# Row sums of banded attention on 64-row tiles in two PSUM banks, with fixed banks in the band steps

## The chip, the cores and the metric

The kernel runs on one core of a Trainium2 chip. TensorE (PE) multiplies matrices and writes only to PSUM, an accumulator memory of eight banks of 512 fp32 columns per partition; VectorE (DVE) and ScalarE (ACT) read PSUM and work elementwise; GpSimd (POOL) works on SBUF; SyncE (SP) issues the transfers. The metric is the time of the whole program on the device in microseconds, a median of runs; lower is better.

## The reference

The input x has the shape (2, 256, 128, 128): batch B, time T, frequency FB, channels C. Three layers follow one another, each with a residual:

```python
xt = _ln(x, ln_t_w, ln_t_b).transpose(0, 2, 1, 3)
x = x + _mha(xt, t_wi, t_bi, t_wo, t_bo, 4, causal_mask(256)).transpose(0, 2, 1, 3)
xf = _ln(x, ln_f_w, ln_f_b)
x = x + _mha(xf, f_wi, f_bi, f_wo, f_bo, 4, band_mask(128, 16))   # |i - j| <= 16
xn = _ln(x, ln_n_w, ln_n_b)
x = x + gelu(xn @ w1.T + b1) @ w2.T + b2                          # 128 -> 512 -> 128
```

All values are fp32. Attention has four heads of 32 channels; a softmax weight is the exponential of a score divided by the sum of the exponentials over the keys. In the second layer a query sees only the keys within 16 places, so a query among the first 48 of 128 sees only the first 64 keys, a query among the last 48 only the last 64, and the 32 in the middle see keys of both halves.

## The kernel before

The work is cut into groups of four tiles of 128 tokens (512 columns). There are three kinds. `OverTime` (128 groups) computes attention over time and comes first. Then follow 16 runs; each has eight `OverBands` groups (attention over frequency, called B1 to B8 here) and then eight `FeedForward` groups (F1 to F8). `run` (line 1263) writes the order of the instructions out by hand: step n issues the first half of group n, the weighted sums (`weigh`) of group n-1, and the output product of group n-2, besides loads and normalisations of later groups and the queries, keys and values of group n+1. Each engine keeps exactly this order (`InOrder`, line 894), and waits on the others by semaphores.

In a band step PE does, in this order: the scores of the group (`OverBands.scores`, line 775: keys times queries, 32-row by 64-column tiles, 80 queries for each half of the keys); the row sums and the weighted values of the group before (`weigh`, line 814: `rp` and `op`); the output product of the one before that (`output`, line 630: `yp`); then the queries, keys and values of the next group (`queries_keys`, `values`). ACT makes the exponentials into the tile `pf`, then for the group before the logarithm of the sums (`ln`) and its exponential (`r`, a first estimate of the reciprocal), then copies queries, keys and values out of PSUM. POOL cuts the band of three heads of `pf` by two selects each; DVE adds the band mask of the fourth to its scores before the exponential ("bank<-bank,band" in the profile). DVE then, in its order: normalises a later group (four "xh"), transposes it ("z"), adds the output to the residual (`finish`, line 636, "x<-bank,x"), and in `divide` (line 615) refines the reciprocal ("bank<-bank,r", "u") and multiplies the weighted values by it ("oT"). In steps B4 to B6 the statistics of F1 to F3 follow, in B8 those of F4; their root (`rstd`) is computed by POOL.

At the turn, step F1, both halves of the hidden products are issued first, then the sums of B8, whose reciprocal is taken exactly (`invert_exactly`, line 610, one DVE RECIPROCAL), then the output of B7 and its `finish`, which stands behind the RECIPROCAL in DVE's order. Step F2 issues half of its hidden products ("xnT,w1f" in the profile), the second product of F1 ("w2T_sb,hT", into `zp`), the other half of the hidden products, and the output of B8.

In the steps of bands and feed-forward every PSUM tile takes the next of the eight banks in turn (`bank`, line 944, and `turn_of_bank`, line 940), with one or two banks set aside ahead for the output and the next queries (`held`, `follow`). A bank that is written again waits for those who still read it. The product that makes all 512 columns of a head's row sums is one matrix multiplication with a matrix of ones: 128 keys, 32 output rows, 512 queries.

Of the kernel before, what the change touches and what calls it, by code (L numbers as in the profile page):

```python
# [19 lines left out]
P = 128  # L20
H = 4
# [11 lines left out]
BANK = 512  # L33
HALF = P // 2
LARGE = 1e20
EXP_SET = "natural_log_exp_and_others"


# [520 lines left out]


class Attention(Group):
    which = None
    swapped = ()
    place = {}
# [6 lines left out]
    def queries_keys(self):  # L571
        path = self.path
        wf = path.k.wf[self.which]
        self.qp = path.bank([P, NT * P], "qp", self.place.get("qp", path.held.pop("qp", None)))
# [27 lines left out]
    def invert(self):  # L602

        path = self.path
        ln = path.work.tile([P, NT * P], F32, name="ln", bufs=2)
        path.scalar.activation(ln, self.rp, AF.Ln)
        self.r0 = path.work.tile([P, NT * P], F32, name="r0", bufs=2)
        path.scalar.activation(self.r0, ln, AF.Exp, scale=-1.0)

    def invert_exactly(self):  # L610
        self.r0 = None
        self.r = self.path.work.tile([P, NT * P], F32, name="ln", bufs=2)
        self.path.vector.reciprocal(self.r, self.rp)

    def divide(self):

        path, vector = self.path, self.path.vector
        if self.r0 is None:
            self.oT = path.work.tile([P, NT * P], F32, name="oT", bufs=2)
            u = path.work.tile([P, NT * P], F32, name="u", bufs=2)  # L620
            vector.tensor_tensor(by_rows(u), by_tile(self.op), by_tile(self.r), ALU.mult)
            vector.tensor_scalar(self.oT, u, -1.0, None, ALU.mult)
            return
        vector.tensor_tensor(self.rp, self.rp, self.r0, ALU.mult)
        u = path.work.tile([P, NT * P], F32, name="u", bufs=2)
        vector.scalar_tensor_tensor(u, self.rp, 2.0, self.r0, ALU.subtract, ALU.mult)
        self.oT = path.work.tile([P, NT * P], F32, name="oT", bufs=2)
        vector.tensor_tensor(by_rows(self.oT), by_tile(self.op), by_tile(u), ALU.mult)

    def output(self):  # L630
        path = self.path
        self.yp = path.bank([P, NT, P], "yp", self.place.get("yp", path.held.pop("yp", None)))
# [9 lines left out]
def rows_of(h):  # L642
    return slice(h * D, (h + 1) * D)
# [124 lines left out]
class OverBands(Attention):  # L768


    which = 1
    follow = ("yp",)
    by_vector = 1

    def scores(self, heads):
        path = self.path
        self.sp = {h: path.bank([P, NT * P], "sp") for h in heads}
        for i in range(NT):
            for e in range(2):
                keys = slice(e * HALF, (e + 1) * HALF)  # L780
                a = i * P + e * (HALF - BAND)
                q = slice(a, a + HALF + BAND)
                for h in heads:
                    r = rows_of(h)
                    path.tensor.matmul(
                        self.sp[h][keys, q], self.kT[r, i * P + e * HALF : i * P + (e + 1) * HALF], self.qT[r, q],
                        start=True, stop=True,
                    )
# [24 lines left out]

    def weigh(self):
        path = self.path

        path.held = {name: path.turn_of_bank() for name in self.follow}
        self.rp = path.bank([P, NT * P], "rp")
        for h in range(H):
            path.tensor.matmul(  # L820
                self.rp[rows_of(h), :], path.k.ones[:, 0:D], self.p[:, h].rearrange("p i q -> p (i q)"),
                start=True, stop=True,
            )
        self.op = path.bank([P, NT * P], "op")
        for i in range(NT):
            c = slice(i * P, (i + 1) * P)
            for h in range(H):
                r = rows_of(h)
                path.tensor.matmul(self.op[r, c], self.v[:, i, r], self.p[:, h, i, :], start=True, stop=True)


class FeedForward(Group):
# [36 lines left out]
    def weigh(self):  # L869
        path, NI = self.path, self.path.k.NI  # L870
        if self.last:
            zp = [path.bank([P, P], "zp") for i in range(NT)]
        else:
            self.zp = path.bank([P, NT, P], "zp")
            zp = [self.zp[:, i] for i in range(NT)]
        self.zps = zp
        for i in range(NT):
            for j in range(NI):
                product(
                    path, zp[i], self.hT[:, j, i * P : (i + 1) * P], path.k.w2T[:, j, :],  # L880
                    start=(j == 0), stop=(j == NI - 1),
                )
# [26 lines left out]
class BoundedPath:  # L909
    def __init__(self, ctx, tc, k):  # L910
        self.tc, self.nc, self.k = tc, tc.nc, k
        self.xpool = ctx.enter_context(tc.tile_pool(name="xpool", bufs=3))
        self.work = ctx.enter_context(tc.tile_pool(name="work", bufs=3))
        self.small = ctx.enter_context(tc.tile_pool(name="small", bufs=6))
        ps = ctx.enter_context(tc.tile_pool(name="ps", bufs=1, space=PSUM))
        self.ps = [ps.tile([P, BANK], F32, name=f"bank{i}", tag=f"bank{i}") for i in range(8)]
        self.next_bank = 0
        self.inputs = 0
        self.held = {}
# [12 lines left out]
        self.band = once.tile([P, P], F32, name="band")  # L932
        tc.nc.gpsimd.memset(self.band, 0.0)
        for s in (1, -1):
            tc.nc.gpsimd.affine_select(
                out=self.band, in_=self.band, compare_op=ALU.is_ge, fill=-1e30, base=BAND,
                pattern=[[-s, P]], channel_multiplier=s,
            )

    def turn_of_bank(self):  # L940
        i, self.next_bank = self.next_bank, (self.next_bank + 1) % 8
        return i

    def bank(self, shape, name, i=None):

# [317 lines left out]
    def run(self, x, out):  # L1263
# [7 lines left out]
        def at(n, kind):  # L1271
            return 0 <= n < len(groups) and isinstance(groups[n], kind)
# [3 lines left out]
                do(n, *names)  # L1276


        for i in range(len(groups) - 2):
            if at(i, OverBands) and at(i + 1, OverBands):  # L1280
                groups[i].follow = ("yp", "qp")
# [15 lines left out]

        ff = [i for i in range(len(groups)) if at(i, FeedForward)][2:]

        self.start(groups)  # L1300
        for n in range(len(groups) + 2):
            feeds = [at(n - 2 + i, FeedForward) for i in range(5)]
# [2 lines left out]
            old, new = (groups[i] if at(i, OverTime) else None for i in (n, n + 1))  # L1305
            if bands[2] and feeds[1]:
                self.scalar.preload_act_table_set(EXP_SET)
            if n + 4 in early:
                do(n + 4, "root")
            do(n, "first_half", "first_function", "first_mask")  # L1310
            if n == 0:
                do(3, "normalize_flat")
            if 2 < n < 6:
# [3 lines left out]
            if old is not None or new is not None:  # L1317
                time_scores(old, new)
                b = self.banks
                Attention.place = dict(yp=b["b0"], rp=b["b3"], op=b["a1"], qp=b["a2"], kp=b["b1"], vp0=b["b0"], vp1=b["b2"])  # L1320
            else:
                Attention.place = {}
            if old is not None:
                old.second_weights(old.late)
                if n + 2 < TURNED:
# [175 lines left out]
```

## Time and profile before

| what | us |
|---|---|
| median of 3 runs | 2636.74 (2636.16 to 2640.02) |
| the profiled execution, its own time | 2633.24 |
| its span, first to last instruction | 2631.4 |
| PE busy | 2618.3 (100%) |
| DVE busy | 2140.6 (81%) |
| ACT busy | 1837.9 (70%) |
| POOL busy | 1956.4 (74%) |
| row sums of bands on PE (pf,ones), 1024 records | 146.8 |
| whole rows of oT on DVE, 240 | 166.0 |
| exact reciprocals on DVE, 16 | 53.1 |
| from one run's reciprocal to the next | 105.5 to 107.4 |

The busy time of an engine is the time in which at least one of its instructions is under way. PE's matrix products are pipelined, so that a product is listed as busy until its last column has left the array, while the next has long begun; the ends are modelled. How fast PE really works is read from the distance between the starts. All instructions carry the line of the helper that issues them (L904), so they are told apart by operation, tile names and shape: "bank<-pf,ones 128*32 128x512" is a product whose moving operand is `pf`, whose weights are the ones, on a tile of 128 rows by 32 columns, with 512 columns moved. An entry in square brackets is the engine's idle time before the row and the engine that ended it. The granted TensorE clock was 1.000 over the span.

### The profile page before, as it was taken

What the parts mean: (1) busy time and instruction counts of PE and PEld (TensorE: products, weight loads), DVE (VectorE), ACT (ScalarE), POOL (GpSimd) and SP (SyncE); (2) the same over time, 40 slices, a digit from 0 to 9 for tenths busy, and PEclk for the clock granted to TensorE, in tenths of its full rate; (3) what the DMA queues carried; (4) which work ended last, traced back from release to release, by engine and by line L of the source; (5) the groups of instructions that cost most, each with busy time, mean ns of one, the idle gap of its engine ahead of it and who ended that gap; (6) DMA issues with size and microseconds to landing.
All of it is one profiled execution on the core that took longest, in us unless ns stands there. A gap on an engine that the chain in (4) does not pass through costs nothing.

```text
span 2631.4 us, 156457 instructions
## 1 busy us (share of the span) xinstructions
PE 2618.3 (100%) x68688; PEld 1862.3 (71%) x68688; DVE 2140.6 (81%) x6410; ACT 1837.9 (70%) x3543; POOL 1956.4 (74%) x2311
## 2 busy tenths in 40 slices
PE   9999999999999999999999999999999999999998
PEld 6666666666666666777777777766677766867776
DVE  8888888888888887977878779778797797887974
ACT  7989989998998875664655746647557466475573
POOL 7999999999999977666667666665776666657762
PEclk9999999999999999999999999999999999999999
DMA  6656556555556454454454444454454445444433
GB/s 156 165 152 156 148 150 158 145 155 155 149 154 152 120 128 119 116 128 118 119 131 123 124 115 123 124 127 116 127 123 122 121 118 130 126 118 121 122 101 87
DMA packets 469845, 344.97 MB, mean 131 GB/s; under 512 B 43168, under 2 KB 404512, under 8 KB 469152
## 3 DMA queue, kind: packets, MB, share of 16 engines
q1 hardware_dynamic: 468432, 334.41, 49.7%
q8 instruction: 540, 8.85, 1.5%
q14 instruction: 153, 1.25, 0.2%
q10 hardware_dynamic: 720, 0.46, 0.1%
HBM read 167.98 MB, written 166.72 MB: 127 GB/s over the span
## 4 chain that ended last, share of the span: by engine, by line
PE 98%; DVE 1%; ACT 0%; issue 0%; DMA 0%; POOL 0%; ACTq 0%; DVEq 0%; POOLq 0%
PE bank L904 98%; DVE xh L904 0%; DVE stats L904 0%; DVE ln L904 0%; ACT hT L904 0%; DMA x<-in_x 0%; DVE z L904 0%; POOL rstd L904 0%; DVE mv L904 0%; DVE x L904 0%; DVE res L904 0%; DVE bank L904 0%; DVE u L904 0%; DVE gs L904 0%; DVE oT L904 0%
## 5 line engine op out<-in xcount | busy, mean ns | idle before, releaser
L904 ACT ACTIVATE hT<-bank,b 128x512 f32<-128x512 f32 x512 | 347.7, 687 | 516.7 <-PE bank L904 464.4
L904 POOL TENSOR_SCALAR_AFFINE_SELECT pf<-pf 128x512 f32<-128x512 f32 x768 | 476.7, 635 | 184.2 <-ACT pf L904 158.0
L904 PEld LDWEIGHTS bank<-w2T_sb,hT 128*32 128x32 f32 x16384 | 475.4, 110 | 48.5 <-issue 17.8
L904 PE MATMUL bank<-xnT,w1f 128*32 128x512 f32 x4096 | 497.0, 592 | 0.0
L904 PE MATMUL bank<-xnT,wf 128*32 128x512 f32 x4096 | 492.0, 592 | 0.5 <-DVE xnT L904 0.5
L904 PE MATMUL bank<-w2T_sb,hT 128*32 128x128 f32 x16384 | 490.1, 273 | 1.1 <-issue 0.6
L904 ACT ACTIVATE p<-bank 128x512 f32<-128x512 f32 (+1 forms) x1024 | 430.3, 495 | 63.4 <-PE bank L904 63.4
L904 DVE TENSOR_SCALAR xh<-x,mv,rstd 128x160 f32<-128x160 f32 (+1 forms) x1012 | 394.7, 434 | 59.5 <-POOL rstd L904 49.3
L904 POOL TENSOR_SCALAR_AFFINE_SELECT p<-p 128x1024 f32<-128x1024 f32 (+2 forms) x384 | 363.8, 948 | 56.0 <-ACT p L904 47.7
L904 PEld LDWEIGHTS bank<-wf,xnT 128*32 128x32 f32 x8192 | 242.8, 110 | 145.2 <-issue 101.5
L904 DVE BATCH_NORM_STATS2 stats<-x 128x6 f32<-128x128 f32 x1536 | 329.3, 278 | 3.3 <-DMA x<-in_x 3.3
L904 POOL TENSOR_TENSOR p<-p,p 128x512 f32<-128x512 f32 x256 | 323.8, 1286 | 10.7
L904 POOL TENSOR_SCALAR rstd<-mv 128x4 f32<-128x4 f32 x251 | 57.3, 228 | 364.9 <-DVE mv L904 363.2
L904 PEld LDWEIGHTS bank<-xnT,w1f 128*32 128x32 f32 x4096 | 203.5, 110 | 158.5 <-issue 79.8
L904 PE MATMUL bank<-qT,kT 32*64 32x80 f32 (+4 forms) x16384 | 302.5, 271 | 0.0
L904 PEld LDWEIGHTS bank<-qT,kT 32*64 32x64 f32 x16384 | 260.2, 131 | 51.4 <-ACT kT L904 50.6
L904 DVE TENSOR_TENSOR res<-bank,res 128x512 f32<-128x512 f32 (+1 forms) x259 | 170.5, 658 | 154.5 <-PE bank L904 151.0
L904 ACT ACTIVATE pf<-bank 128x512 f32<-128x512 f32 x512 | 265.8, 603 | 38.2 <-PE bank L904 37.6
L904 PE MATMUL bank<-wn,oT 128*32 128x128 f32 x8192 | 287.2, 274 | 0.3 <-issue 0.2
L904 DVE STREAM_TRANSPOSE z<-xh 128x512 f32<-128x512 f32 x380 | 270.4, 712 | 13.3
L904 PE MATMUL bank<-wf,xnT 128*32 128x128 f32 x8192 | 276.2, 273 | 0.0
L904 POOL TENSOR_TENSOR rstd<-rstd,mhalf 128x4 f32<-128x4 f32 x251 | 260.6, 1038 | 20.9
(100 smaller groups left out, 3832.6 us busy)
## 6 DMA issues: line engine op xcount, KB each, us to landing
turned<-z SPq DMA_DIRECT2D x1520, 64.0 KB, 2.6
xnT<-turned SPq DMA_DIRECT2D x380, 256.0 KB, 3.0
x<-res SPq DMA_DIRECT2D x256, 128.0 KB, 2.4
x<-x SPq DMA_DIRECT2D x128, 256.0 KB, 3.9
out<-res SPq DMA_DIRECT2D x252, 128.0 KB, 2.3
x<-in_x SPq DMA_DIRECT2D x124, 256.0 KB, 4.2
x<-in_x SPq DMA_DIRECT2D x4, 128.0 KB, 2.8
x<-in_x SPq DMA_DIRECT2D x6, 64.0 KB, 2.7
```

The source lines that it names most:

```text
L904: return self.tc.keep_in_program_order(emit(*args, **kwargs))
```

## The change

The row sums of a band group are split. For each head, the outer 48 queries of each half are summed over the 64 keys of that half alone (a 64-row tile, 48 queries of each of four tiles of tokens: 192 columns), and the 32 middle ones, 16 for each half, over all 128 keys (64 columns). The two halves of the queries (e = 0, 1) go to two neighbouring banks, 4 and 5, 256 columns in each; so the sums of a head take four products in place of one. The sums now lie in the order half, tile, query, and `like_sums` and `in_sums` bring the operands of ACT and DVE into that order; the multiplication that makes oT is issued in two halves of 256 columns.

Because banks 4 and 5 are now one tile, all banks in these steps are fixed: the scores in 3, 2, 0, 1; in a band step the output in 3, the queries in 2, the keys in 0; the weighted values and the next group's values in 7 and 6, changing places from step to step. In the feed-forward steps `turns` sets an order of banks at F1, at F2 and at F8. And the root for a later feed-forward group is issued after the masks of the step, no longer ahead of them.

```diff
+PAIR = 4, 5
+SCORES = 3, 2, 0, 1
+SIDES = 7, 6
...
 class Attention(Group):
+    @staticmethod
+    def like_sums(t):
+        return t
+    in_sums = like_sums
...
-        path.scalar.activation(ln, self.rp, AF.Ln)
+        path.scalar.activation(self.like_sums(ln), self.rp, AF.Ln)
...
-        self.path.vector.reciprocal(self.r, self.rp)
+        self.path.vector.reciprocal(self.in_sums(self.r), self.rp)
...
-        vector.tensor_tensor(by_rows(self.oT), by_tile(self.op), by_tile(u), ALU.mult)
+        self.multiply(by_rows(self.oT), by_tile(self.op), u)
...
 class OverBands(Attention):
+    @staticmethod
+    def like_sums(t):
+        return t.rearrange("p (e i q) -> p e i q", e=2, i=NT)
+    @staticmethod
+    def in_sums(t):
+        return t.rearrange("p (i e q) -> p e i q", e=2, i=NT)
+    def multiply(self, to, op, u):
+        for e, half in enumerate((u[:, 0 : BANK // 2], u[:, BANK // 2 :])):
+            t = slice(2 * e, 2 * e + 2)
+            self.path.vector.tensor_tensor(to[:, :, t], op[:, :, t], by_tile(half), ALU.mult)
...
-        self.sp = {h: path.bank([P, NT * P], "sp") for h in heads}
+        self.sp = {h: path.bank([P, NT * P], "sp", SCORES[h]) for h in heads}
...
     def weigh(self):
-        path.held = {name: path.turn_of_bank() for name in self.follow}
-        self.rp = path.bank([P, NT * P], "rp")
+        self.rp = path.pair[:, :, 0 : BANK // 2].rearrange("p e (i q) -> p e i q", i=NT)
+        alone = HALF - BAND
         for h in range(H):
-            path.tensor.matmul(
-                self.rp[rows_of(h), :], path.k.ones[:, 0:D], self.p[:, h].rearrange("p i q -> p (i q)"),
-                start=True, stop=True,
-            )
-        self.op = path.bank([P, NT * P], "op")
+            for e in range(2):
+                keys = slice(e * HALF, (e + 1) * HALF)
+                path.tensor.matmul(
+                    self.rp[rows_of(h), e, :, e * BAND : e * BAND + alone], path.k.ones[keys, 0:D],
+                    self.p[keys, h, :, e * (P - alone) : e * (P - alone) + alone], start=True, stop=True,
+                )
+        for h in range(H):
+            for e in range(2):
+                path.tensor.matmul(
+                    self.rp[rows_of(h), e, :, (1 - e) * alone : (1 - e) * alone + BAND], path.k.ones[:, 0:D],
+                    self.p[:, h, :, alone + e * BAND : HALF + e * BAND], start=True, stop=True,
+                )
+        self.op = path.bank([P, NT * P], "op", self.place.get("op"))
...
-            self.zp = path.bank([P, NT, P], "zp")
+            self.zp = path.bank([P, NT, P], "zp", Attention.place.get("zp"))
...
     def turn_of_bank(self):
-        i, self.next_bank = self.next_bank, (self.next_bank + 1) % 8
+        i, self.next_bank = self.order[self.next_bank], (self.next_bank + 1) % len(self.order)
         return i
+    def turns(self, *banks):
+        self.order, self.next_bank = list(banks), 0
...
+        side = list(SIDES)
+        s, pair = SCORES, PAIR
+        def places(n):
+            place = {}
+            if at(n, OverBands):
+                place = dict(yp=s[0], qp=s[1], kp=s[2])
...
+                else:
+                    if at(n - 1, FeedForward):
+                        place.update(zp=pair[0])
+                    place.update(op=side[0], vp=side[1])
+                    if at(n + 1, OverBands):
+                        side.reverse()
+            elif at(n, FeedForward):
+                if at(n - 1, OverBands):
+                    place = dict(op=side[1], yp=side[0])
+                    self.turns(*s)
+                elif at(n - 2, OverBands):
+                    self.turns(s[0], s[1], side[0], s[2], s[3], *pair, side[1])
+                elif not at(n + 1, FeedForward):
+                    self.turns(*s, side[0], *pair, side[1])
+                    side.reverse()
+            return place
...
+            if old is None:
+                Attention.place = places(n)
+            do(n, "first_half", "first_function", "first_mask")
             if n + 4 in early:
                 do(n + 4, "root")
-            do(n, "first_half", "first_function", "first_mask")
```

More of the change, by code (lines that the diff above doesn't have):

```diff
@@ L573, in queries_keys @@
         wf = path.k.wf[self.which]
-        self.qp = path.bank([P, NT * P], "qp", self.place.get("qp", path.held.pop("qp", None)))
+        self.qp = path.bank([P, NT * P], "qp", self.place.get("qp"))
         product(path, self.qp, wf[:, 0:P], self.xnT)
@@ L623, in divide @@
             return
-        vector.tensor_tensor(self.rp, self.rp, self.r0, ALU.mult)
+        r0 = self.like_sums(self.r0)
+        vector.tensor_tensor(self.rp, self.rp, r0, ALU.mult)
         u = path.work.tile([P, NT * P], F32, name="u", bufs=2)
-        vector.scalar_tensor_tensor(u, self.rp, 2.0, self.r0, ALU.subtract, ALU.mult)
+        vector.scalar_tensor_tensor(self.like_sums(u), self.rp, 2.0, r0, ALU.subtract, ALU.mult)
         self.oT = path.work.tile([P, NT * P], F32, name="oT", bufs=2)
-        vector.tensor_tensor(by_rows(self.oT), by_tile(self.op), by_tile(u), ALU.mult)
+        self.multiply(by_rows(self.oT), by_tile(self.op), u)
+    def multiply(self, to, op, u):
+        self.path.vector.tensor_tensor(to, op, by_tile(u), ALU.mult)
     def output(self):
         path = self.path
-        self.yp = path.bank([P, NT, P], "yp", self.place.get("yp", path.held.pop("yp", None)))
+        self.yp = path.bank([P, NT, P], "yp", self.place.get("yp"))
         for i in range(NT):
@@ L771, with multiply @@
     which = 1
-    follow = ("yp",)
     by_vector = 1
+    @staticmethod
[4 more added lines that the diff above has]
+        return t.rearrange("p (i e q) -> p e i q", e=2, i=NT)
+    def multiply(self, to, op, u):
+        for e, half in enumerate((u[:, 0 : BANK // 2], u[:, BANK // 2 :])):
+            t = slice(2 * e, 2 * e + 2)
+            self.path.vector.tensor_tensor(to[:, :, t], op[:, :, t], by_tile(half), ALU.mult)
     def scores(self, heads):
         path = self.path
-        self.sp = {h: path.bank([P, NT * P], "sp") for h in heads}
+        self.sp = {h: path.bank([P, NT * P], "sp", SCORES[h]) for h in heads}
         for i in range(NT):
@@ L915, in __init__ @@
         ps = ctx.enter_context(tc.tile_pool(name="ps", bufs=1, space=PSUM))
-        self.ps = [ps.tile([P, BANK], F32, name=f"bank{i}", tag=f"bank{i}") for i in range(8)]
-        self.next_bank = 0
+        self.pair = ps.tile([P, 2, BANK], F32, name="pair", tag="pair")
+        self.ps = [
+            self.pair[:, i - PAIR[0]] if i in PAIR else ps.tile([P, BANK], F32, name=f"bank{i}", tag=f"bank{i}")
+            for i in range(8)
+        ]
+        self.order, self.next_bank = list(range(8)), 0
         self.inputs = 0
-        self.held = {}
         self.banks = dict(zip(("a1", "a2", "b0", "b3", "a0", "a3", "b1", "b2"), range(8)))
@@ L1276, in do_at @@
                 do(n, *names)
-        for i in range(len(groups) - 2):
-            if at(i, OverBands) and at(i + 1, OverBands):
-                groups[i].follow = ("yp", "qp")
         run0 = [i for i in range(len(groups)) if at(i, OverBands)][: RUN // NT]
@@ L1298, in run @@
         ff = [i for i in range(len(groups)) if at(i, FeedForward)][2:]
+        side = list(SIDES)
[4 more added lines that the diff above has]
+                place = dict(yp=s[0], qp=s[1], kp=s[2])
+                if at(n - 1, OverTime):
+                    place.update(rp=pair[0], op=side[1], vp=side[0])
+                elif at(n - 2, OverTime):
+                    place.update(op=side[1], vp=side[0])
+                else:
[14 more added lines that the diff above has]
+            return place
         self.start(groups)
@@ L1320, in run @@
                 Attention.place = dict(yp=b["b0"], rp=b["b3"], op=b["a1"], qp=b["a2"], kp=b["b1"], vp0=b["b0"], vp1=b["b2"])
-            else:
-                Attention.place = {}
+                if new is None:
+                    Attention.place.update(qp=SCORES[0], kp=PAIR[0], vp=SIDES[0])
             if old is not None:
```

## The prediction

> **What bounds the kernel now.** I read the page first: its busy shares and its chain.
>
> ```profile
> PE 2618.3 (100%) x68688; PEld 1862.3 (71%) x68688; DVE 2140.6 (81%) x6410; ACT 1837.9 (70%) x3543; POOL 1956.4 (74%) x2311
> ...
> PE 98%; DVE 1%; ACT 0%; issue 0%; DMA 0%; POOL 0%; ACTq 0%; DVEq 0%; POOLq 0%
> ```
>
> TensorE (PE) is never seen idle for long, and the chain that ended last runs through it. A microsecond taken from PE is won, and a microsecond of PE waiting is lost, unless another engine decides at that place. So next I took the timeline of PE in a band step (steps B1 to B8 are the eight band groups of a run, F1 to F8 its eight feed-forward groups; one run goes from about 1245 to 1351 us; columns: start, length, engine, operation, tiles, shape, count).
>
> ```profile
> 1257.86 0.97 PE L904 MATMUL bank<-qT,kT 32*64 32x80 f32 x64
> 1258.76 1.06 PE L904 MATMUL bank<-pf,ones 128*32 128x512 f32 x8
> 1259.64 1.06 PE L904 MATMUL bank<-pf,v 128*32 128x128 f32 x32
> ...
> 1264.09 0.97 PE L904 MATMUL bank<-qT,kT 32*64 32x80 f32 x64
> ```
>
> A step lasts 6.23 us, and its row sums (pf,ones) last 0.88 us from their start to that of the next product. The groups kept apart by shape give the rate (after the bar: busy us, mean ns of one):
>
> ```profile
> L904 PE MATMUL bank<-p,v 128*32 128x256 f32 x2048 | 157.4, 379 | 0.0
> ...
> L904 PE MATMUL bank<-pf,ones 128*32 128x512 f32 x1024 | 146.8, 603 | 0.0
> L904 PE MATMUL bank<-p,ones 128*32 128x256 f32 x2048 | 134.0, 379 | 0.0
> ```
>
> The 603 mixes 592 ns with 617 ns for the first of each phase. (592 - 379) / 256 columns is 0.83 ns per column. Every product is recorded twice, so it makes two passes: 2 x 512 x 0.83 = 853 ns, nearly all of the 0.88 us. The single records show that the four heads run side by side on four column tiles and start 6 to 7 ns apart; and that wherever the tile shape changes (32*64 to 128*32 or back) about 90 to 96 ns pass between the end of the last column and the next start, some 380 times in the kernel. In this run these changes are PE's only gaps.
>
> Then VectorE (DVE), since it hands banks back to PE:
>
> ```profile
> 1265.24 0.70 DVE L904 SCALAR_TENSOR_TENSOR bank<-bank,band 128x512 f32<-128x512 f32 x1 [0.63 <-PE bank L904]
> ...
> 1293.26 0.66 DVE L904 TENSOR_TENSOR x<-bank,x 128x512 f32<-128x512 f32 x1
> ...
> 1300.80 3.32 DVE L904 RECIPROCAL ln<-bank 128x512 f32<-128x512 f32 x1
> 1304.04 0.63 DVE L904 TENSOR_TENSOR x<-bank,x 128x512 f32<-128x512 f32 x1
> ...
> 1305.30 0.43 DVE L904 TENSOR_SCALAR oT<-u 128x512 f32<-128x512 f32 x1
> ```
>
> From 1265.24 (step B4) DVE works without a pause up to oT, but for one 1.48 us wait for POOL's rstd at 1298.52, because four steps carry the statistics of later groups besides. I call this **the vector chain**. In all sixteen runs it has the same offsets to 10 ns: the first x<-bank,x ends 6.87 us before the reciprocal starts, the second 3.87 us after. PE meanwhile:
>
> ```profile
> 1293.02 3.60 PE L904 MATMUL bank<-xnT,w1f 128*32 128x512 f32 x30
> ...
> 1300.44 3.67 PE L904 MATMUL bank<-w2T_sb,hT 128*32 128x128 f32 x122
> ```
>
> F1's hidden products start before 1293.02 (the first tile at 1292.68, the slower two tiles at 1293.02), and F2's step starts its w2T products at 1300.44 (slower tiles 1300.77), while DVE still has to read two banks of outputs at 1293.92 and 1304.67. Today that costs nothing: the rotation gives PE other banks there.
>
> **The row sums on PE.** The new phase has eight outer products of 192 columns on 64-row tiles and eight middle ones of 64 columns on 128-row tiles. No 64*32 tile is in the trace; the nearest row is the scores, where eight tiles on four row groups start 6 to 7 ns apart and write four banks at once. So I take the outer ones as eight at a time: first weight load 25 ns (617 - 592), two passes of 160 ns, stagger of the eighth tile 46 ns: 391. Then the shape changes once more, 90. Middle: 25 for the load, four rounds of 58 ns (64-column scores in the time stage repeat on one tile after 58 ns), 40 for the stagger, since two products of one tile follow each other: 297. In sum 778 ns, against 883 plus 20 of stagger: **0.125 us less**. If the halves did not overlap, outer would take 320 ns more and the step would lose 0.2 us; if the extra shape change and the stagger vanished, 0.26 us would be won. I take 0.125, the value made of rows.
> Here the Trainium skill speaks against the change. "PSUM — Partial Sum Buffer" (section Specifications) warns that any non-contiguous access pattern slows matmuls significantly, and the new outputs come in runs of 48 and 16 columns. The rows above are against it: p,ones writes and reads two separate runs of 128, p,v one run of 256, both 379 ns. By the rows the sum stays; were a short run to double the time, 0.55 us per step would be lost. Runs of 16 are not in the trace, so I keep a little of that in the range.
> 112 of the 128 sums stand after scores; the 16 at F1 stand between 128*32 phases, where two shape changes instead of none eat the gain (868 against 873 ns). PE's own gain: 112 x 0.125 = 14 us.
>
> **The vector work.** oT becomes two halves. A whole one lets the next instruction start after 0.61 us, 512 columns at the 1.04 ns per column that 0.69 us against 0.425 us (one 256-column sum of this kind) give, plus 0.08. Two of 256: 2 x 0.345 = 0.69, so +0.08 us (0.06 to 0.15). The other like_sums operands only reorder columns; ln, r, u keep 512 columns: nothing. Of the chain's divides five get the extra: +0.40.
>
> **The moved root.** POOL's rstd work for F1 to F3 now follows the masks of its step. Today the masks of B7 run 1286.40 to 1290.33 behind an rstd that waited 1.29 us, and the sums at 1290.06 of two heads are late for it: this is the 0.33 us lag of two tiles. Masks come earlier, the lag goes; rstd comes about 3 us later, near 1289.5, and is wanted by xh at 1290.99, so it is covered; without that cover it would delay DVE by what is missing. No DMA is moved.
>
> **The fixed banks, in the band steps.** Sums always in 4 and 5: free after u. At B8 u ends 1289.75 and the sums start 1290.06; with PE earlier and DVE later PE waits there up to 0.5 us, only down to DVE's pace. The other banks I followed one by one (scores 3, 2, 0, 1; yp 3, qp 2, kp 0; 7 and 6 in turn): each is read at least 0.5 us before reuse, but bank 3 before B8's scores, about 0.1 us short.
>
> **The fixed banks, at the turn.** Here it goes wrong.
> First hand-over: B8's output goes to bank 3 (yp=s[0]), and the next thing on PE is F1's first hidden product, whose order was just reset to start at s[0]: bank 3. It must wait for x<-bank,x, which follows band, four xh and z on DVE. The chain shifts by two sums before its anchor (B2, B3: -0.25) and four halved divides (+0.32): 1293.92 + 0.07 + 0.05 (DVE's end to PE's start, as oT 1305.73 to 1305.78) = 1294.04. PE would be ready near 1292.3: 1.7 us idle. Behind it on PE's queue stands everything.
> Second: at F1 the output goes to side[0], and in the next step the third bank in the order, F2's zp, is side[0] again. Its reader is the x<-bank,x at 1304.04, behind the 3.32 us reciprocal. 1304.67 + 0.15 (-0.25 + 0.40) + 0.05 = 1304.87. PE, from 1294.04: 3.44 hidden, 0.87 sums, 0.87 and 0.87 products, 1.72 hidden: ready at 1301.8. It stands for 3.0 us, and the w2T products start at 1304.87 where the slower tiles now start at 1300.77: **+4.10 us per run**. All of PE's gains in the run, the lag and the first wait are inside this figure, for the vector chain, not PE, sets this time. DVE does not wait for PE in it: the sums of F1 end by 1298.6 and are wanted at 1300.95. From there PE again never waits (hidden, output and later banks were read long before, and oT is long ready).
>
> **Sum.** 16 x 4.10 = 65.6 us. Span 2631.4 + 65.6 = 2697.0; the profiled execution took 2633.24, 1.84 more than its span: 2698.8. The median of the runs lies 3.5 above it, 2636.74: **2702.3 us**.
> The second rule: "TensorE: Matmul & The Clock Gate" (Part 1) says that an idle window of about 3.4 us halves PE's clock. The page grants full clock in all 40 slices, but after the start no wait there is so long. A 3.0 us stand is shorter than the rule's window, so by rule and row nothing is added. If a nearly idle window is enough, up to 3.4 us at half rate cost 1.7 us per turn, estimated from that page: +27 us.
>
> **Rivals.** (1) Only the first hand-over bites, the second bank being free in time: then zp starts at 1301.83, +1.06 per run, 17 us: 2654. For it: PE has few waits today, so a wait of 3 us at a fixed place would be new. Against: the bank list names side[0] twice.
> (2) The clock drops after the stand: 2729. For it: 3.0 is close to 3.4. Against: both waits are shorter.
> (3) No hand-over bites, the vector chain alone decides: F2's wn,oT products wait for oT (1305.73, slower tiles today 1305.98). Per run 0.40 - 0.25 - 0.20 = -0.05: 2636, no change.
> (4) Faster: PE's gain comes through. Place: both hand-overs; it decides when the readers end before PE comes, that is when x<-bank,x stands 1.7 and 3.0 us earlier than the chain has it, and oT 0.6. Price: -14 us, 2623. For it: PE bounds 98% of the chain. Against: DVE's order isn't touched.
>
> **Chances.** Forecast 0.62, (1) 0.12, (2) 0.14, (3) 0.04, (4) 0.08. Alone, the forecast's range is 2690 to 2715 (chain shift -0.05 to +0.6, times 16). Eight in ten: from below (1) to (2), 2650 to 2735. A change of 0.2%, 5 us, is about what this measurement can tell. Slower 0.88, same 0.04, faster 0.08.
>
> **What would show it.** PE's busy time stays near 2605 to 2620 while its idle time grows to some 75 us, ended by DVE x; the first w1f product of a run starts 0.05 us after x<-bank,x; the w2T products of F2 start about 4.0 us after the reciprocal starts, not 0.36 before; sums take about 0.76 us to the first pf,v; oT appears twice with 256 columns. The step that would make me wrong is the reading of the bank order at F1 and F2, or a DVE order other than today's.

## The result, and the profile after

The kernel with the change takes **3041.65 us** (median of 4 runs, 3037.08 to 3051.23) against 2636.45 before: ratio **1.1535**, 95% interval 1.152 to 1.1549. It is slower by 405 us; the forecast was 2702, with a range of 2650 to 2735. The profiled execution spans 3049.1 us. Its page, the busy shares and the chain:

```profile
PE 2728.1 (89%) x71760; PEld 1848.6 (61%) x71760; DVE 2165.0 (71%) x6522; ACT 1831.5 (60%) x3543; POOL 1956.0 (64%) x2311
...
PE 70%; DVE 17%; ACT 5%; POOL 4%; issue 3%; DMA 0%; DVEq 0%; SPq 0%; ACTq 0%; POOLq 0%
```

PE, idle for 13 us in all before, is now idle for 11% of a longer span, and the chain goes through DVE, ACT and POOL: PE waits for others. What PE waits for (us in total, times, longest):

```profile
PE pair L936 <- DVE oT L936: 64.6, 43, 2.0
PE bank L936 <- DVE x L936: 60.6, 32, 2.8
PE pair L936 <- DVE x L936: 48.5, 16, 3.9
PE pair L936 <- DVE res L936: 36.7, 38, 1.0
PE pair L936 <- ACT p L936: 33.1, 43, 1.0
PE bank L936 <- issue: 29.5, 47, 1.3
PE pair L936 <- DVE vy L936: 12.0, 11, 1.6
PE pair L936 <- POOL p L936: 10.6, 10, 1.1
```

Only the second row, two waits in each of 16 runs, was in the forecast. The rows with "pair" belong to the tile that banks 4 and 5 have become. All the waits for oT, p, vy and POOL's p, and 21 of the 38 for res, lie in a stage in which the change edits no step: attention over time. By stage (window; its length, then busy us of PE, PEld, DVE, ACT, POOL, with instructions; granted clock, share of DMA, GB/s), first before, then after:

```profile
20.00:923.00 903.00, 902.92 (x24346) 625.61 (x24348) 769.58 (x2299) 812.27 (x1849) 836.28 (x767) 1.00 0.59 151
923.00:2631.00 1708.00, 1698.88 (x44120) 1225.79 (x44110) 1357.97 (x4042) 1015.21 (x1672) 1110.89 (x1524) 1.00 0.48 120
```

```profile
20.00:1114.00 1094.00, 950.26 (x24360) 649.79 (x24362) 780.64 (x2298) 812.72 (x1850) 837.83 (x768) 0.98 0.49 125
1114.00:3049.00 1935.00, 1761.22 (x47182) 1188.23 (x47174) 1371.09 (x4153) 1008.68 (x1672) 1108.78 (x1522) 0.97 0.43 106
```

The time stage lost 191 us: PE stood for 144 us (before: none) and was busy 47 us longer for the same products, in part because of the clock: the trace has ten stretches of 3.41 us at half clock there, in which PE was busy for 34 us, so some 17 us are lost. The rest was not parted; the tail of a product before a stand counts as busy. The sixteen runs lost 227 us: 165 more idle, 62 more busy. In them 29 such lengths of 3.41 us at half clock hold 88 us of busy time, some 44 us lost. One such place in PE's timeline in the time stage:

```profile
403.90 1.08 PE L936 MATMUL pair<-wn,oT 128*32 128x128 f32 x32 [0.76 <-ACT p L936]
405.98 1.07 PE L936 MATMUL pair<-p,ones 128*32 128x256 f32 x16 [1.01 <-DVE res L936]
```

The table of banks of the time stage (`hand_banks_on`) gives bank 5 to this group's output (wn,oT) and bank 4 to the row sums (p,ones) after it. DVE reads the output into res:

```profile
405.14 0.69 DVE L936 TENSOR_TENSOR res<-pair,res 128x512 f32<-128x512 f32 x1 [0.34 <-PE pair L936]
```

The sums start at 405.98, just after that reading, although they write the other bank. And the turn of a run, PE and then DVE:

```profile
1288.32 3.64 PE L936 MATMUL bank<-xnT,w1f 128*32 128x512 f32 x32 [0.86 <-DVE x L936]
...
1299.13 5.37 PE L936 MATMUL bank<-w2T_sb,hT 128*32 128x128 f32 x128 [2.84 <-DVE x L936]
...
1309.34 1.37 PE L936 MATMUL pair<-xnT,w1f 128*32 128x512 f32 x8 [2.26 <-DVE x L936]
```

```profile
1287.57 0.69 DVE L936 TENSOR_TENSOR x<-bank,x 128x512 f32<-128x512 f32 x1 [0.83 <-PE bank L936]
...
1295.20 3.32 DVE L936 RECIPROCAL ln<-pair 128x512 f32<-128x512 f32 x1
1298.44 0.63 DVE L936 TENSOR_TENSOR x<-bank,x 128x512 f32<-128x512 f32 x1
...
1308.63 0.66 DVE L936 TENSOR_TENSOR x<-pair,x 128x512 f32<-128x512 f32 x1
```

The two hand-overs of the forecast stand as they were described: F1's hidden products start 0.06 us after x<-bank,x ends, and the w2T products 3.93 us after the reciprocal's start. Two things were not in it: in 8 of the 16 turns, this one among them, those w2T products last 5.1 to 5.4 us where they lasted 3.67; and a third stand follows, of F3's hidden products, which go to one half of the pair (bank 5) while DVE has still to read the output of B8 from the other (x<-pair,x). Its length is 2.3 to 3.9 us in 15 of the 16 turns. The sums themselves, kept apart by shape (busy us, mean ns):

```profile
L936 PE MATMUL pair<-pf,ones 64*32 64x192 f32 x2048 | 74.6, 335 | 1.8 <-issue 1.6
L936 PE MATMUL pair<-pf,ones 128*32 128x64 f32 x2048 | 61.0, 225 | 2.4 <-issue 2.2
```

From their start to that of the values they take 0.734 us (median of 128) where it was 0.882.

### The profile page after: what moved, and what is told of

It reads as the page before. It is cut to its first block, busy times and chain, and to the rows that moved or that the text cites. A ratio compares the mean times of both kernels' runs of the same rounds, so it can differ in the third digit from the quotient of the medians.

```text
span 3049.1 us, 162911 instructions
## 1 busy us (share of the span) xinstructions
PE 2728.1 (89%) x71760; PEld 1848.6 (61%) x71760; DVE 2165.0 (71%) x6522; ACT 1831.5 (60%) x3543; POOL 1956.0 (64%) x2311
## 4 chain that ended last, share of the span: by engine, by line
PE 70%; DVE 17%; ACT 5%; POOL 4%; issue 3%; DMA 0%; DVEq 0%; SPq 0%; ACTq 0%; POOLq 0%
PE bank L936 52%; PE pair L936 18%; ACT p L936 3%; DVE xh L936 3%; POOL p L936 2%; DVE stats L936 2%; DVE u L936 2%; DVE oT L936 2%; DVE ln L936 2%; DVE bank L936 1%; DVE res L936 1%; POOL rstd L936 1%; DVE z L936 1%; DVE x L936 1%; DVE mv L936 1%
## 5 line engine op out<-in xcount | busy, mean ns | idle before, releaser
L936 ACT ACTIVATE hT<-bank,b 128x512 f32<-128x512 f32 x418 | 285.4, 688 | 452.1 <-PE bank L936 446.4
L936 PE MATMUL bank<-xnT,wf 128*32 128x512 f32 x3512 | 436.4, 592 | 1.5 <-ACT r L936 0.8
L936 DVE TENSOR_SCALAR xh<-x,mv,rstd 128x160 f32<-128x160 f32 (+1 forms) x1012 | 394.0, 431 | 56.4 <-POOL rstd L936 47.2
L936 PEld LDWEIGHTS bank<-w2T_sb,hT 128*32 128x32 f32 x12224 | 357.1, 115 | 118.3 <-DVE x L936 59.9
L936 PE MATMUL bank<-xnT,w1f 128*32 128x512 f32 x3344 | 400.7, 607 | 15.2 <-DVE x L936 15.2
L936 PE MATMUL bank<-w2T_sb,hT 128*32 128x128 f32 x12224 | 373.6, 283 | 45.4 <-DVE x L936 45.4
L936 DVE TENSOR_TENSOR res<-bank,res 128x512 f32<-128x512 f32 x183 | 123.8, 677 | 338.9 <-PE bank L936 270.2
L936 ACT ACTIVATE p<-bank 128x512 f32<-128x512 f32 (+1 forms) x767 | 329.8, 500 | 42.0 <-PE bank L936 32.8
L936 PE MATMUL bank<-wf,xnT 128*32 128x128 f32 x7520 | 264.3, 273 | 0.0
L936 PE MATMUL bank<-wn,oT 128*32 128x128 f32 x6336 | 224.9, 274 | 13.2 <-issue 12.3
L936 PEld LDWEIGHTS bank<-xnT,w1f 128*32 128x32 f32 x3344 | 107.1, 112 | 210.7 <-issue 181.7
```

The source lines that it names most:

```text
L936: return self.tc.keep_in_program_order(emit(*args, **kwargs))
```

## The experiments

Four theories. **A**: waits are kept per tile, so one tile of two banks makes the users of bank 4 wait for those of bank 5, everywhere. **B**: the fixed banks make the two hand-overs, worth some 65 us. **C**: the sums make 12 more products per band step, and PE's supply of instructions runs dry. **D**: PE's clock falls after stands and adds to some of them. "Minus before" is against the median of the kernel before on the same chip (2634.97, 2637.58 and 2632.45 in the three groups).

| kernel | us | ratio (95%) | minus before |
|---|---|---|---|
| before, banks 4 and 5 one tile | 2988.11 | 1.1338 (1.1303 to 1.1373) | +353.1 |
| fixed banks, old sums, eight tiles | 2709.92 | 1.0282 (1.0252 to 1.0312) | +75.0 |
| the change, two orders at the turn mended | 2869.47 | 1.0888 (1.0856 to 1.0919) | +234.5 |
| split sums, pair joined late, turn mended | 2682.18 | 1.0177 (1.0147 to 1.0207) | +47.2 |
| before, sums as 16 products | 2663.64 | 1.0106 (1.0087 to 1.0125) | +26.1 |
| split sums, F4 and F8 mended too | 2673.09 | 1.0131 (1.0111 to 1.0152) | +35.5 |
| fixed banks, only the second hand-over freed | 2653.80 | 1.0058 (1.0038 to 1.0078) | +16.2 |
| fixed banks, only the first freed | 2730.41 | 1.0349 (1.0328 to 1.0369) | +92.8 |
| fixed banks, both freed | 2632.50 | 1.0002 (0.9993 to 1.001) | 0.0 |
| before, root after the masks | 2630.60 | 0.9992 (0.9983 to 1.0) | -1.9 |
| the same, and DVE's order at F1 | 2625.53 | 0.9973 (0.9963 to 0.9984) | -6.9 |

**One tile alone.** The kernel before, with nothing but the allocation changed:

```diff
-        self.ps = [ps.tile([P, BANK], F32, ...) for i in range(8)]
+        self.pair = ps.tile([P, 2, BANK], F32, name="pair", tag="pair")
+        self.ps = [self.pair[:, i - 4] if i in (4, 5) else ps.tile([P, BANK], F32, ...) for i in range(8)]
```

> The kernel before with one edit: banks 4 and 5 are allocated as one PSUM tile of two banks; sums, bank rotation and order stay. Theory A (shared tile: who uses one half of the two-bank tile waits for the users of the other half, though they touch another bank): the time stage, where nothing else was changed, ends near 1114 us as after the change and not near 923 us as before, and more is lost in the runs, in all 2830 to 3000 us. Theory B (only the fixed bank order at the turn costs, as predicted): the tile is harmless, 2636 us within 0.2%.

Measured: +353 us, with the same products in the same order and the same turn of banks. The first band scores start at 1104.5 us against 923.5, so 181 us are lost in the time stage. PE's waits:

```profile
PE pair L904 <- DVE oT L904: 69.2, 45, 2.2
PE pair L904 <- DVE res L904: 34.7, 36, 1.0
PE pair L904 <- ACT p L904: 33.1, 43, 1.0
PE pair L904 <- DVE x L904: 28.1, 22, 1.9
PE pair L904 <- DVE u L904: 27.7, 5, 6.3
```

Before, PE had no such wait. Theory A is shown. In the runs of this kernel the tile stands in the turn of all eight banks, so its stands there are not those of the change; in the time stage they are the same.

**Fixed banks alone.** The change with the sums put back (one product for each head, in bank 4) and eight tiles:

```diff
-        self.rp = path.pair[:, :, 0 : BANK // 2].rearrange(...)   # and the 16 products
+        self.rp = path.bank([P, NT * P], "rp", PAIR[0])           # and the 4 products as before
-        self.pair = ps.tile([P, 2, BANK], F32, name="pair", tag="pair")
```

> The changed kernel with eight separate banks and the old row sums (one product of 512 columns per head into bank 4 alone, oT in one piece); the fixed banks, the orders at F1, F2 and F8 and the moved root stay. Theory B: two waits at each turn, first w2T product of F2 about 3.9 us after the reciprocal starts in place of 0.36 us before it; 16 x 4.0 = 64 us, and some 1.6 us per turn more if the clock drops after the stand of 3 us: 2695 to 2730 us. Theory A alone: 2636 us.

Measured: +75.0 us. PE's waits name one cause, and the turn shows both stands of the forecast:

```profile
PE bank L914 <- DVE x L914: 61.8, 32, 2.8
...
1306.95 3.64 PE L914 MATMUL bank<-xnT,w1f 128*32 128x512 f32 x32 [1.09 <-DVE x L914]
...
1317.69 3.70 PE L914 MATMUL bank<-w2T_sb,hT 128*32 128x128 f32 x128 [2.78 <-DVE x L914]
```

In all 16 turns the w2T products start 3.92 to 3.93 us after the reciprocal. From the first of the 128 to the last they take 3.43 us in eight turns and mostly 5.1 (once 4.83) in the other eight, at the same stand. A run with a fast turn lasts 109.6 us, 3.9 more than the usual 105.72 before. 16 x 3.9 + 8 x 1.65 = 75.6: theories B and D together give the measured 75.

**The turn mended in the change.**

```diff
-                    self.turns(*s)
+                    self.turns(s[1], s[2], s[3], s[0])
...
-                    self.turns(s[0], s[1], side[0], s[2], s[3], *pair, side[1])
+                    self.turns(s[1], s[2], s[3], s[0], pair[0], side[0], pair[1], side[1])
```

> The changed kernel with other bank orders at F1 (2, 0, 1, 3) and F2 (2, 0, 1, 3, 4, side, 5, side), so that no product at the turn takes a bank whose reader stands late on DVE; the two-bank tile stays. Theory B: the waits of F1's first hidden product and of F2's w2T products go, 16 x (4.1 + up to 3 for the clock) less: 2930 to 2975 us. Theory A alone: the time stays within 1% of 3042 us, its first band step still near 1114 us.

Measured: some 171 us less than the change (234.5 over before in place of 405), more than expected, since the third stand (48.5 us of waits) and the waits for res in the runs (15.6 us) go too and the mean clock rises from 0.977 to 0.995: one length of 3.41 us at half clock is left in the runs, where the change had 29. The time stage stays slow (first band scores at 1106.6), and so do the waits of the pair for oT, p and res: A again.

**Split sums without the shared tile in the time stage.** Banks 4 and 5 are two tiles until the bands begin, then one; the orders at the turn use the pair for little else than the sums:

```diff
+            (low if i in PAIR else ps).tile([P, BANK], F32, ...) for i in range(8)
...
+    def join_pair(self, ctx):
+        self.early.close()
+        high = ctx.enter_context(self.tc.tile_pool(name="high", bufs=1, space=PSUM))
+        self.pair = high.tile([P, 2, BANK], F32, name="pair", tag="pair")
```

> The changed kernel with the split sums, where the time stage uses banks 4 and 5 as two tiles; only from the first band step on they are one tile, and there little but the sums is put into it; orders at the turn as in the run before. If A and B are all that costs, PE's stands go: time stage ends near 923 us, and the total is bounded by the vector chain at the turn (2636 us) or below it by the 14 us of the shorter sums: 2615 to 2645 us. If the split sums or the operands over two banks cost something themselves, it stays above 2660 us.

Measured: +47.2, with the time stage back at 924.0. Two things remained: 15 waits at F4, 16 us in all, which came from my own order of banks there, and short stands that no engine ends.

**F4 and F8 mended.** The same, with this order at F4, and others at F3 and F8 to go with it:

```diff
+                elif at(n - 4, OverBands):
+                    self.turns(pair[0], s[1], side[0], side[1], s[2], s[0], s[3])
```

> The split sums with the late two-bank tile as in e4, with the orders of banks from F4 and at F8 changed so that F4's first hidden product no longer takes the bank of F2's output. By the stands in e4's trace (1.28 us before that product in each run): 16 x 1.28 = 20 us less than e4, 2662 us. If that stand only covered another wait: no change from 2682 us.

Measured: +35.5, still slower than before, though the sums are 0.15 us shorter per step and of the waits for other engines less than 4 us are left after the start:

```profile
PE bank L936 <- issue: 21.5, 39, 1.7
PE pair L936 <- issue: 4.0, 13, 0.5
...
1276.96 0.30 PE L936 MATMUL bank<-pf,v 128*32 128x128 f32 x2 [0.39 <-issue]
```

"issue" is waiting for nothing that the profile shows. To count all of them, I take the time from one product's start to the next beyond what nearly all (the 99th percentile, the 90th for rare ones) such pairs of products take, where it is 0.18 us or more. Laid beside the DMA records, such stands are not random: of 70, half end between 1.31 and 1.46 us after the end of a 16-KB transfer on the instruction queue; there are 566 such transfers, 540 before. They stand inside phases too, where no tile shape changes and no bank is taken. Together these stands take 40.5 us, against 4.9 in the same stretch before.

**More products, nothing else.** The kernel before, its sums cut in four along the queries:

```diff
-        for h in range(H):
-            path.tensor.matmul(self.rp[rows_of(h), :], ..., self.p[:, h].rearrange("p i q -> p (i q)"), ...)
+        for i in range(NT):
+            for h in range(H):
+                path.tensor.matmul(self.rp[rows_of(h), i * P : (i + 1) * P], ..., self.p[:, h, i, :], ...)
```

> The kernel before with one edit: the row sums of bands are sixteen products of 128 columns (four per head) in place of four of 512; columns, banks and all else stay. Theory C (instruction supply: a band step then holds 104 products on PE as after the change, not 92, and PE runs dry where a block of instructions is fetched too late): PE stands here and there in the band steps with nothing to wait for, each time ending 1.2 to 1.7 us after the end of an instruction fetch, in sum 20 to 40 us: 2655 to 2680 us. Theory D (the number of products is free as long as the columns stay): 2635 us within 0.2%, sums still 0.88 us.

Measured: +26.1 us. (In the text just above, "Theory D" stands for its own rival, that the number of products is free, and not for the clock.) The page counts 71760 products, as many as the change. The sums themselves grew from 0.882 to 0.897 us, 2 us in all; the rest is elsewhere:

```profile
PE bank L905 <- issue: 10.3, 23, 1.1
...
1276.31 0.53 PE L905 MATMUL bank<-pf,ones 128*32 128x128 f32 x11 [0.66 <-issue]
1284.62 0.96 PE L905 MATMUL bank<-wn,oT 128*32 128x128 f32 x27 [0.36 <-issue]
```

The same offset: half of its 45 stands, 19.5 us in all, end 1.31 to 1.47 us after an instruction transfer. The transfers go with PE: 3072 more records of products and as many of weight loads, 6144 instructions, come with 24 more transfers (564 against 540), one for 256. That the number of products costs time beyond their columns is shown; that the supply of instructions is the reason is the reading that fits the offsets; no run changed the supply itself, so it is not shown. If it is right, the Trainium skill is too hopeful here: "Runtime: NRT & Kernel Launch" (Instruction fetch mechanics) says that an engine's instructions come in blocks of 16 KB and that crossing a block is mostly hidden. At 92 products per band step the stands are few (14, 4.9 us in all); at 104 they are not.

**Which hand-over costs.** Fixed banks with one of the two orders mended: first only F2's,

```diff
-                    self.turns(s[0], s[1], side[0], s[2], s[3], *pair, side[1])
+                    self.turns(*s, pair[1], side[0], pair[0], side[1])
```

> e2 (fixed banks, old sums, separate tiles) with only the order at F2 changed (3, 2, 0, 1, 5, side, 4, side), so that F2's w2T products take a bank that is long free; F1's first hidden product still takes bank 3. By the step model: one wait of 1.2 us per turn is left, no stand over 2 us, clock full: 16 x 1.0 to 1.3 = 16 to 21 us over before, 2651 to 2657 us. If the first wait is hidden too: 2635 us.

Measured: +16.2. Then only F1's:

```diff
-                    self.turns(*s)
+                    self.turns(s[1], s[2], s[3], s[0])
```

> e2 with only the order at F1 changed (2, 0, 1, 3), so that F1's first hidden product no longer waits; F2's w2T products still take the bank of F1's output. By the step model the vector chain sets when they start, so the first wait is inside the second: PE stands 4.1 to 4.3 us there in place of 1.2 and 2.95, and the time is that of e2, 2710 us within 5 us, or more if the longer stand costs more clock (up to 2730 us). If the two waits add up: 2690 us.

Measured: +92.8, more than with both. With the first wait gone, PE arrives earlier at the second and stands longer there:

```profile
1324.47 3.70 PE L914 MATMUL bank<-w2T_sb,hT 128*32 128x128 f32 x128 [3.84 <-DVE x L914]
```

The start is still 3.92 us after the reciprocal: DVE sets it, so the first wait costs nothing beside the second. The longer stand (3.8 to 4.3 us in 15 turns, 2.65 in one) costs clock: 14 of 16 turns are slow now (4.96 to 6.23 us), not 8. And both:

> The fixed banks of the change with the sums as before (one product per head, bank 4) and eight separate banks, but with both orders at the turn mended: F1 takes banks 2, 0, 1, 3 and F2 takes 2, 0, 1, 3, 4, the side bank, 5, the other side bank. If the two hand-overs are all that the fixed banks cost, the time comes back to that of the kernel before, 2636 to 2642 us, the first band scores start at 924 to 925 us, and no wait of PE for DVE's x is left above 0.3 us. If the fixed banks also cost something in the band steps or in F3 and F4, it stays at 2650 or more. The distance from this kernel to the one with split sums and mended turns (2673) is then what the split sums themselves cost, 30 to 37 us.

Measured: 2632.50 against 2632.45 before. The fixed banks cost nothing in the band steps; all of their 75 us came from the orders at F1 and F2. Beside this kernel, the split sums with their two-bank tile and mended turns (+35.5) cost 35 us net.

**The moved root.** The one part of the change left, alone:

```diff
+            do(n, "first_half", "first_function", "first_mask")
             if n + 4 in early:
                 do(n + 4, "root")
-            do(n, "first_half", "first_function", "first_mask")
```

> The kernel before with one part of the change alone: the root for a later feed-forward group is issued after the masks of the step. The forecast held that the lag of 0.33 us that two of the four column tiles have at the turn goes, and that the later root is covered. If the lag is worth something, up to 5 us are won (2631 to 2637); if DVE's xh at 1290.99 waits for the later root and PE waits for DVE, up to 1 us per run is lost (2640 to 2653); no difference if the turn is set by the chain of DVE.

Measured: -1.9 us, within what can be told from no change. The lag of two column tiles at the turn is gone, as foreseen, and the usual run shortens from 105.72 to 105.5 us.

**DVE's order at F1.** In addition DVE's normalisation of the group three ahead, at F1, goes behind the divide, so that both x<-bank,x and oT come earlier:

```diff
-            do_at(n + 3, (OverBands, FeedForward), "normalize", "turn")
+            if not turn:
+                do_at(n + 3, (OverBands, FeedForward), "normalize", "turn")
...
             do(n - 1, "divide")
+            if turn:
+                do_at(n + 3, (OverBands, FeedForward), "normalize", "turn")
```

> The kernel before with the root after the masks, and besides at F1 the normalisation and transposition of the group three ahead moved behind the divide on DVE, so that the output of B7 is read and oT is ready some 3 us earlier. If the chain of DVE at the turn holds PE up at all, this frees it: 2629 to 2635 us. If PE alone sets the turn, the time is that of the kernel before within 0.2%; if the delayed normalisation is late for F4's hidden products, 2640 or more.

Measured: 2625.53 us, ratio 0.9973 (0.9963 to 0.9984). The usual run takes 105.24 us. Its turn:

```profile
1294.37 3.36 DVE L904 RECIPROCAL ln<-bank 128x512 f32<-128x512 f32 x1
1297.64 0.63 DVE L904 TENSOR_TENSOR x<-bank,x 128x512 f32<-128x512 f32 x1
...
1298.90 0.43 DVE L904 TENSOR_SCALAR oT<-u 128x512 f32<-128x512 f32 x1
```

```profile
1302.79 1.06 PE L904 MATMUL bank<-wn,oT 128*32 128x128 f32 x32
```

oT now ends 3.5 us before PE's product needs it; before it was 0.05 us, which fits that DVE had held PE up a little at this place all along.

## Why the prediction was wrong

The direction was right, and the 65.6 us of its sum were found; the size was wrong by 340 us. Step by step:

- **The step that failed: banks 4 and 5 counted as two tiles.** The description of the change says that they are one, and each reader of either half is a condition for each writer of either half. Where the forecast looked, this did no harm: "Sums always in 4 and 5: free after u" holds, since the sums in the pair wait for no other engine in the changed kernel. It failed at two places. No term stands for the time stage, put at nothing without a reason because no step of it is edited; but it takes its banks from the same eight, and it lost 191 us, 144 of them in stands of PE. And "From there PE again never waits (hidden, output and later banks were read long before ...)": at F3 PE stood in every run, 48.5 us in all, and in later feed-forward steps 15.6 us for res, all at the pair; neither wait occurs with the same orders and eight tiles. With two tiles in the time stage, that stage is back at 924.0; with the orders at the turn mended, both waits of the runs are gone.
- **The two hand-overs: right.** Forecast 4.10 us per run; measured 3.9 in turns without loss of clock. The w2T products start at 3.92, forecast 4.00. The first stand was 1.7 in the forecast and 0.9 to 1.4 in the runs, which changes nothing, since the second contains it. Rival (1), only the first hand-over biting, was forecast at +17 us; the kernel made that way, with the old sums, has +16.2.
- **The clock: the wrong value taken.** "By rule and row nothing is added", and 1.7 us per turn as the alternative. With fixed banks and the old sums a stand of 2.8 us does halve the rate, in half of the turns, at 1.65 us each: 13 us where 0 was taken and 27 was the other end. The price worked out from the page of the Trainium skill ("TensorE: Matmul & The Clock Gate", Part 1: one window of 3.4 us at half rate) was right; the limit taken from it, that a shorter stand costs nothing, was not. The same part says that the window runs freely, whatever the program does, and the trace agrees: the stretches at half clock last 3.41 us, or two or three times that, and within one execution all begin on one grid of 3.41 us (last section). So the same stand costs or does not by where it falls on the grid. In the whole kernel the clock costs more, since there are more stands: some 61 us, half of the 122 us in which PE was busy at half clock.
- **The row sums: right in size, wrong in effect.** 0.15 us less per step, forecast 0.125; the runs of 48 and 16 columns cost nothing that shows (335 ns for a product of 192 columns on 64 rows, 225 for one of 64; the scores of the time stage, with as many columns, 329 and 223). But the step counted columns and shape changes, not instructions. Twelve more products per step cost 26 us where they are made alone, more than the 19 us (128 x 0.149) that the shorter sums give. So even without A and B the split does not pay. Of the 35 us net, the stands of 0.18 us or more account for 35 (40.5 less 5.5 in the kernel with both hand-overs freed), and 35 - 19 = 16; the other 19 I could not assign to a row. The "some 380" shape changes of the forecast are 509 in the trace before; its sum does not use them.
- **The moved root and oT in halves: right.** The lag went; the two halves take 0.75 us for 0.69.

How the parts stand to the whole, in the profiled execution, which is 418 us longer than that of the kernel before: the time stage 191; in the runs the two hand-overs 61, the third stand 48, the waits for res 16, stands that no engine ends 32, other waits some 8, and 62 of longer busy time, of which the clock is some 44.

## What to carry to other kernels

Ask of every buffer that an edit merges, splits or renames who else takes it, in stages the diff does not touch, and count each merged one as a single lock: its cost is read from the waits of its old users, not from the new code. An edit that makes products smaller has to be priced in instructions as well as in columns when PE is the bound. Several waits on one chain cost what the last of them costs, so mending the first alone can make things worse.

## What the runs showed of the hardware that was not expected

- In the kernel with fixed banks and old sums PE stands for 2.8 us in each of 16 turns, and its clock is halved in 8 of them. A turn at full clock and one at half clock, each the window of the grid that holds most of the stand and the window after it (columns as in the stage tables above; the clock stands before the share of DMA):

```profile
1315.72:1319.14 3.42, 1.45 (x53) 1.45 (x57) 3.39 (x7) 0.00 (x0) 0.00 (x0) 1.00 0.26 46
1319.14:1322.55 3.41, 3.41 (x100) 2.51 (x95) 1.90 (x10) 0.23 (x1) 2.62 (x4) 1.00 0.52 151
1424.95:1428.36 3.41, 1.05 (x40) 1.05 (x44) 3.38 (x5) 0.33 (x1) 0.00 (x0) 1.00 0.42 100
1428.36:1431.77 3.41, 3.41 (x76) 3.38 (x68) 1.94 (x11) 0.00 (x0) 2.23 (x3) 0.50 0.44 108
```

- In this run the eight windows that come just before one at half clock were busy for 18 to 39%, and every other window between the start and the end for 42% or more. Over the five kernels here whose clock fell between their start and end, a window at full clock was always followed by half clock when PE was busy for up to 39% of it and never when for 49% or more; between the two both occur. A window at half clock was followed by another up to 77%, and by full clock from 84%. (The ends of products are modelled, so the shares are rough.) The runs don't show how to tell beforehand where the grid lies, so a forecast should carry the fall as a chance: 8 of 16 turns here, 14 of 16 with stands of about 4 us.
- The fall comes late: in the turn of the changed kernel shown above, products of one tile start every 0.109 us for the first 0.6 us, and then every 0.21 us for some 3.3 us.
- With 104 instead of 92 products in a band step of 6.2 us, PE stands for 0.2 to 1.7 us at a time, typically 1.3 to 1.5 us after the end of a 16-KB instruction transfer.
